# A stack of four graph-attention layers: the minimum over adj moved, a's columns scaled on GpSimd and fetched first, the last batch finished one tile at a time

## The chip, the cores and the metric

The kernel runs on one core of a Trainium2 chip. A core has five engines with instruction queues of their own: TensorE (PE in the profile; its weight loads are PEld), VectorE (DVE), ScalarE (ACT), GpSimd (POOL) and SyncE (SP), which here issues nearly all transfers. Each engine works through its queue in order and waits on semaphores that the others raise. The metric is the time of the whole launch on the device in microseconds, the median of several runs. Less is better.

## The reference

Input x has 32 batches of 512 nodes with 256 features, in float32; adj is a 512 x 512 matrix of int32, zeros and ones in these inputs, with ones on its diagonal. Four layers follow one another, each added to x:

```python
h = relu(layernorm(x)); x = x + L0(h, adj, W, a)   # one head, slope 0.2, elu
h = relu(layernorm(x)); x = x + L1(h, adj, W, a)   # one head, slope 0.01, relu
h = relu(layernorm(x)); x = x + L2(h, adj, W, a)   # four heads of 64, slope 0.2, elu
h = relu(layernorm(x)); x = x + L3(h, adj, ...)    # see below

# what each attention computes
Wh  = h @ W
e   = leaky_relu(Wh @ a[:F] [:, None] + Wh @ a[F:] [None, :], slope)
e   = where(mask, e, -inf)          # L0: adj > 0 or i == j; L1, L2: adj != 0; L3's last: adj > 0
out = softmax(e, -1) @ Wh           # then elu or relu

# L3
o = relu(h @ mlp1_w + mlp1_b)                     # 256 -> 512
o = elu(elu(gat(o, no mask, W_fc, a_fc))) + o     # all 512 nodes with all
r = relu(o @ mlp2_w + mlp2_b)                     # 512 -> 256
L3 = relu(elu(elu(gat(r, adj > 0, W_hand, a_hand))) + r)
```

In every masked layer a node attends to the nodes that adj names; since the inputs have no negative entries in adj and a full diagonal, one mask serves all layers. (In the reference elu is applied inside gat and again after it.)

## The kernel before

**Two programs.** `fast` computes everything under the assumptions that adj has no negative entry, that its diagonal is positive, and that no exponential grows too large. It leaves a flag. Each engine then loads that flag (L1187) and branches at L1188; only when the flag is set does the slower function `general` compute the output anew. In these runs the flag is clear. Three numbers make up the flag: the minimum over adj (L225 and L226, into `differ[:, 0:1]`), the minimum over the diagonal (L228 and L229), and the largest exponential seen in any batch (`seen`, filled by `note` at L305).

**Layout.** The 512 nodes are four tiles of 128 rows (`NT = 4`), features lie in the free dimension. The exponential of a leaky ReLU of a sum is written as a product: three extra columns beside each W (the columns of `a` projected through W, scaled by slope - 1 and by 1 - slope) give per-node factors, so that a weight is max(row factor, column factor) times the mask. `weights` (L342) makes the four 128 x 512 tiles of weights on VectorE at L352; `aggregate` (L380) multiplies them with the values on PE; a column beside the values (each node's own factor) yields the denominator, and `reciprocal` (L384, instruction at L386) inverts it. The products are float32; PE works through one in two records of the profile.

**Loading.** `load_x` (L93) fetches a batch. `fetch_w` (L128) fetches a weight matrix and calls `fetch_a` (L99), which fetches the two halves of the vector `a` as columns of single floats: two transfers for each layer, issued on SP at L103. SP's order at the start is x of batch 0 (L150), W0 and then its `a` (L151), adj (L153), x of batches 1 to 3, and then the other weights. `finish_w` (L137) scales the columns of `a` (`scale_a`, L109: two instructions on VectorE, for W0, W1, WFC and WHA) and then projects them through W (`project`, L113: transposes on PE, a copy `wT` on ScalarE at L120, small products with `a`, and a copy into the spare columns of W on VectorE at L126).

**The mask.** `setup` (L206) is a generator whose pieces are placed among the first pieces of the batches. It compares adj with zero into `own` (L209, VectorE), puts ones on the diagonal (L210, affine_select on GpSimd), turns the 16 blocks on PE (L218) and stores `maskT` (L219, ScalarE). Then come W1's columns, the minimum over adj, the diagonal's minimum, the columns of W2 (`A`, L231 and L232), WFC's columns, two triangles (`before`, `after`) and the band of ties that a sort uses (L239 to L250), and WHA's columns.

**Order.** Four batches run interleaved (`NS = 4`). Each is a generator (`batch`, L729) that yields a due time after each piece, and the loop at L754 always takes the piece that is due first. A scheduler of the framework then places each engine's instructions by its own estimates of time; `keep_in_program_order` ties an instruction to its place. So program order is not the order of the queues: the triangles' memsets, for instance, stand in VectorE's queue ahead of batch 0's statistics.

**The end of a batch.** `layer3` (L689) ends with a loop over pairs of tiles (`t0` = 0 and 2). For both tiles of a pair the attention's average is taken (`averages`, L396), its exponential and its ReLU are written into the two halves of `q` and `y` (L698, L699), then `elu2_plus1` (L407) makes the double elu over the whole pair: a min on VectorE (L409), an exp on ScalarE (L410), a sum on VectorE (L411). The residual `rT` is transposed on PE into a bank and added (L709, VectorE), ReLU follows (L710, ScalarE), then the addition to x (L712, GpSimd) and the transfer of two tiles to the output (L713, SP, 256 KB). In batches 0 to 30 other batches' work surrounds this; in the last batch nothing follows it but the flag (L774 to L783).

Of the kernel before, what the change touches and what calls it, by code (L numbers as in the profile page):

```python
# [24 lines left out]
OP = mybir.AluOpType  # L25
AX = mybir.AxisListType

EPS = 1.0e-5
P = 128
# [6 lines left out]
def fast(ctx, tc, flag, x, adj, w0, a0, w1, a1, w2, a2, mlp1_w, mlp1_b, mlp2_w, mlp2_b,  # L36
         w_fc, a_fc, w_hand, a_hand, out):
    nc = tc.nc
    B, N, F = x.shape
    NT = N // P  # L40
# [27 lines left out]
    def transpose(p, x, i, tied=False):  # L68
        spent[0] += 2 * P
        instruction = nc.tensor.transpose(p, x, i)  # L70
        if tied:
            tc.keep_in_program_order(instruction)
# [4 lines left out]
    def bank():  # L77

        own = [turn[0], *(i for i in range(NS) if i not in active and i != turn[0])]
        banks[0] += 1  # L80
        return psum.tile([P, N], FP, tag=f"b{own[banks[0] % len(own)]}", name="b", bufs=8 // NS)
# [11 lines left out]
    def load_x(b):  # L93
        t = work.tile([P, NT, F], FP, tag="x", name="x", bufs=NS + 1)
        nc.sync.dma_start(t, x[b].rearrange("(t p) f -> p t f", p=P))
        return t


    def fetch_a(a, name):  # L99
        ft = a.shape[0] // (2 * P)  # L100
        t = const.tile([P, ft, 3], FP, name=name)
        for s, c in ((0, 2), (1, 0)):
            nc.sync.dma_start(  # L103
                t[:, :, c:c + 1],
                a[s * ft * P:(s + 1) * ft * P, :].rearrange("(t p) o -> p t o", p=P),
            )
        return t

    def scale_a(t, alpha):  # L109
        nc.vector.tensor_scalar_mul(t[:, :, 1:2], t[:, :, 0:1], alpha - 1.0)  # L110
        nc.vector.tensor_scalar_mul(t[:, :, 2:3], t[:, :, 2:3], 1.0 - alpha)

    def project(dst, block, k, a_cols):  # L113

        ft, n = a_cols.shape[1], a_cols.shape[2]
        p = bank()
        for f in range(ft):
            transpose(p[:, f * P:(f + 1) * P], block(k, f), ident)
        wT = work.tile([P, N], FP, tag="y", name="wT", bufs=3)
        nc.scalar.copy(wT[:, :ft * P], p[:, :ft * P])  # L120
        q = bank()
        for f in range(ft):
            matmul(
                q[:, :n], wT[:, f * P:(f + 1) * P], a_cols[:, f, :], start=(f == 0), stop=(f == ft - 1)
            )
        nc.vector.tensor_copy(dst, q[:, :n] if len(dst.shape) == 2 else q[:, :n].rearrange("p (h c) -> p h c", c=3))  # L126

    def fetch_w(w, a, name):  # L128

        kt, cols = w.shape[0] // P, w.shape[1]  # L130
        t = const.tile([P, kt, cols + 3], FP, name=name)
        wr = w.rearrange("(k p) f -> p k f", p=P)
        for c in range(0, cols, F):
            nc.sync.dma_start(t[:, :, c + (3 if c else 0):c + (3 if c else 0) + F], wr[:, :, c:c + F])
        return t, fetch_a(a, name + "a")

    def finish_w(fetched, alpha):  # L137
        t, a_cols = fetched

        def block(k, f):  # L140
            c = f * P + (3 if f * P >= F else 0)
            return t[:, k, c:c + P]

        scale_a(a_cols, alpha)
        for k in range(t.shape[1]):
            project(t[:, k, F:F + 3], block, k, a_cols)
            yield


    xts = {0: load_x(0)}  # L150
    W0, _ = fetched0 = fetch_w(w0, a0, "W0")  # L151
    adj_sb = work.tile([P, NT, N], I32, tag="w", name="adj", bufs=4)
    nc.sync.dma_start(adj_sb, adj.rearrange("(t p) j -> p t j", p=P))  # L153
    for b in range(1, NS):
# [1 line left out]
    W1, _ = fetched1 = fetch_w(w1, a1, "W1")  # L156
# [6 lines left out]
    for h in range(NH):  # L163
        t, r = divmod(h * D, P)
# [8 lines left out]
    WFC, _ = fetched3 = fetch_w(w_fc, a_fc, "WFC")  # L173
    WM2 = const.tile([P, KH, F], FP, name="WM2")
    nc.sync.dma_start(WM2, mlp2_w.rearrange("(k p) f -> p k f", p=P))
    WHA, _ = fetched4 = fetch_w(w_hand, a_hand, "WHA")
# [23 lines left out]
    differ = const.tile([P, 2], FP, name="differ")  # L200
# [5 lines left out]
    def setup():  # L206

        own = work.tile([P, NT, N], FP, tag="w", name="own", bufs=4)
        nc.vector.tensor_scalar(own, adj_sb, 0.0, None, op0=OP.is_gt)  # L209
        nc.gpsimd.affine_select(  # L210
            out=own, in_=own, pattern=[[P, NT], [-1, N]], base=0, channel_multiplier=1,
            compare_op=OP.not_equal, fill=1.0,
        )
        for j in range(NT):
            turn[0] = NS - 1 - j % (NS - 1)
            p = bank()
            for t in range(NT):
                transpose(p[:, t * P:(t + 1) * P], own[:, t, j * P:(j + 1) * P], ident, j + t == 0)  # L218
            nc.scalar.copy(maskT[:, j, :], p)  # L219
        turn[0] = NS - 1  # L220
        yield
        yield from finish_w(fetched1, 0.01)


        tc.keep_in_program_order(nc.vector.tensor_reduce(differ[:, 0:1], adj_sb, AX.XY, OP.min))  # L225
        nc.vector.tensor_scalar(differ[:, 0:1], differ[:, 0:1], 0.0, None, op0=OP.is_lt)  # L226
        least = small([1], "rden")
        nc.vector.tensor_reduce(least, diag, AX.X, OP.min)  # L228
        nc.vector.tensor_scalar(differ[:, 1:2], least, 0.0, None, op0=OP.is_le)  # L229
        nc.vector.tensor_copy(W2[:, :, :, :D], raw2.rearrange("p k (h d) -> p k h d", d=D))  # L230
        nc.vector.tensor_scalar_mul(A2v[:, :, 1:2], A2v[:, :, 0:1], -0.8)  # L231
        nc.vector.tensor_scalar_mul(A2v[:, :, 2:3], A2v[:, :, 2:3], 0.8)  # L232
        for k in range(KF):
            project(W2[:, k, :, D:], lambda k, f: raw2[:, k, f * P:(f + 1) * P], k, A2)
            yield
        yield from finish_w(fetched3, 0.2)

        for tri, sign in ((before, 1), (after, -1)):
            nc.vector.memset(tri, 1.0)  # L239
            nc.gpsimd.affine_select(  # L240
                out=tri, in_=tri, pattern=[[sign, P]], base=0, channel_multiplier=-sign,
                compare_op=OP.is_gt, fill=0.0,
            )
        ties = work.tile([P, 2 * N - P], FP, tag="w", name="ties", bufs=4)
        nc.vector.memset(ties, TINY)
        nc.gpsimd.affine_select(
            out=ties, in_=ties, pattern=[[-1, 2 * N - P]], base=N - P, channel_multiplier=1,
            compare_op=OP.is_gt, fill=0.0,
        )
        nc.vector.tensor_copy(band, ties)  # L250
        yield
        yield from finish_w(fetched4, 0.2)
# [3 lines left out]
    def small(shape, name):  # L256
        return work.tile([P] + shape, FP, tag=name, name=name, bufs=2 * NS)
# [33 lines left out]
    def turned(xn, when):  # L291

        hT = work.tile([P, KF, N], FP, tag="hT", name="hT", bufs=3)
        turn_pair(xn, hT, 0)
        yield when
        turn_pair(xn, hT, 2)
        yield after_us(0.6)
        return hT
# [78 lines left out]
    def pair(tag="y"):  # L377
        return work.tile([P, 2, F], FP, tag=tag, name=tag, bufs=3)
# [17 lines left out]
    def averages(v, wt, t):  # L396
        p = bank()
        aggregate(p[:, :F + 1], wt, t, lambda j: v[:, j, :F + 1])
        return p[:, :F], reciprocal(p[:, F:F + 1])
# [289 lines left out]
    def layer3(xt, xn, when, b):  # L689
        oT = yield from linear_t((yield from turned(xn, when)), WM1, b1, "oT", 2)  # L690
        yield from (attend if b >= B - 1 else sort_attend)(oT, b)
        rT = yield from linear_t(oT, WM2, b2, "rT", 2)
        v, wt = yield from plain(rT, WHA)
        for t0 in range(0, NT, 2):
            y, q = pair(), pair("q")
            for i in range(2):
                p, rd = averages(v, wt, t0 + i)
                nc.scalar.activation(q[:, i, :], p, AF.Exp, scale=rd)  # L698
                nc.scalar.activation(y[:, i, :], p, AF.Relu, scale=rd)  # L699
                yield after_us(0)  # L700
            elu2_plus1(y, q)
            p = bank()
            for i in range(2):
                for k in range(KF):
                    transpose(
                        p[:, (i * KF + k) * P:(i * KF + k + 1) * P], rT[:, k, (t0 + i) * P:(t0 + i + 1) * P], ident
                    )
            yf = y.rearrange("p a f -> p (a f)")
            nc.vector.scalar_tensor_tensor(yf, p, -1.0, yf, op0=OP.add, op1=OP.add)  # L709
            nc.scalar.activation(y, y, AF.Relu)  # L710
            xr = xt[:, t0:t0 + 2, :]
            nc.gpsimd.tensor_tensor(xr, xr, y, op=OP.add)  # L712
            nc.sync.dma_start(  # L713
                out[b, t0 * P:(t0 + 2) * P, :].rearrange("(t p) f -> p t f", p=P), xr
            )
            yield after_us(0)

# [36 lines left out]
    while ready:  # L754
        i = min(ready, key=ready.get)
# [23 lines left out]
    p = bank()  # L779
# [437 lines left out]
```

## Time and profile before

| | |
|---|---|
| median of 3 runs | 2943.76 us (2943.12 to 2945.2) |
| the profiled run, whole | 2945.59 us |
| span of the profile | 2943.9 us |
| mean granted clock of TensorE | 0.995 |
| adj landed; own (L209) begins | 10.99 us |
| own's affine_select on GpSimd (L210) | 12.29, for 1.91 us |
| first transposes of WFC on PE | 28.77 us |
| last of the output transfers (256 KB each) issued | 2938.5 us |

All times in the trace are microseconds from the start of the span. A line of the timeline gives start, duration, engine, line of the kernel, operation, output and inputs by their names, and in brackets how long the engine had been idle before it and what released it. The page's chain is followed back from the last instruction: at each step to whatever released it, or to the instruction before it in the same queue; its lines give the share of the span that each engine or line holds on this chain. The start and the end of the span differ from its middle in that few batches are under way: from 10 to 20 us PE is busy for 8.6 of 10 us, and after 2932 us for 0.4 us in all.

### The profile page before, as it was taken

How to read it: one execution, taken by the hardware profiler on the slowest of the kernel's cores; microseconds unless marked ns; L12 is line 12 of the kernel's file. 1: busy time of each engine (PE TensorE's matmuls, PEld its weight loads, DVE VectorE, ACT ScalarE, POOL GpSimd, SP SyncE). 2: the span in 40 equal slices, each digit the busy share in tenths (PEclk: the TensorE clock that was granted, in tenths of full speed). 3: DMA queues.
4: the chain of work that ended last, by engine and by line, in shares of the span. 5: the costliest groups of instructions: out<-in, count | busy, mean ns of one | idle time of the engine just before them, and what ended most of it. 6: DMA issues, size and time to landing. Idle time of an engine off the chain costs nothing.

```text
span 2943.9 us, 43065 instructions
## 1 busy us (share of the span) xinstructions
PE 2863.2 (97%) x15177; PEld 2326.1 (79%) x15177; DVE 2224.0 (76%) x5674; ACT 1537.4 (52%) x3918; POOL 501.3 (17%) x509
## 2 busy tenths in 40 slices
PE   7999999999999999999999999999999999999988
PEld 6777888877887877888878888778888788887766
DVE  4677877778877778878777878777777788787764
ACT  4444455554555554555554555545555555555544
POOL 0011112111122111122021121121221111221120
PEclk9999999999999999999999999999999999999999
DMA  3033223233223233233332232332232322332230
GB/s 94 19 101 99 87 83 116 92 96 99 90 87 105 95 98 98 83 102 98 98 101 90 86 107 93 96 99 89 87 116 89 99 95 81 101 112 77 96 106 23
DMA packets 193150, 270.89 MB, mean 92 GB/s; under 512 B 16992, under 2 KB 156062, under 8 KB 192928
## 3 DMA queue, kind: packets, MB, share of 16 engines
q1 hardware_dynamic: 163168, 169.76, 18.5%
q0 software_dynamic: 29760, 98.30, 10.1%
q8 instruction: 123, 2.02, 0.3%
q14 instruction: 99, 0.81, 0.1%
HBM read 152.62 MB, written 115.39 MB: 91 GB/s over the span
## 4 chain that ended last, share of the span: by engine, by line
PE 77%; DVE 13%; ACT 5%; DMA 3%; issue 1%; POOL 0%; SPq 0%; POOLq 0%; ACTq 0%; DVEq 0%
PE b L66 70%; PE b L70 7%; DVE st L268 3%; DVE xn L279 1%; DMA order<-v,at 1%; DVE xn L275 1%; DVE sums L640 1%; DVE w L352 1%; ACT v L324 1%; DMA sums<-order 1%; DVE sums L631 1%; ACT y L504 1%; DVE x L405 1%; ACT q L503 1%; DVE y L404 1%
## 5 line engine op out<-in xcount | busy, mean ns | idle before, releaser
L66 PE MATMUL b<-v,w 128*128 128x65 f32 (+1 forms) x7232 | 1222.4, 321 | 6.8 <-DVE w L352 6.7
L66 PEld LDWEIGHTS b<-v,w 128*128 128x128 f32 x7232 | 1053.6, 192 | 167.8 <-issue 64.2
L66 PE MATMUL b<-WFC,oT 128*128 128x256 f32 (+1 forms) x2048 | 496.3, 380 | 0.0
L66 PEld LDWEIGHTS b<-WFC,oT 128*128 128x128 f32 x2048 | 373.6, 189 | 48.7
L66 PE MATMUL b<-W,hT 128*128 128x259 f32 (+1 forms) x1536 | 382.0, 387 | 9.2 <-ACT hT L289 4.4
L352 DVE SCALAR_TENSOR_TENSOR w<-b,v,maskT 128x512 f32<-128x512 f32 x512 | 369.0, 743 | 4.9 <-PE b L70 3.6
L606 POOL DMA_INDIRECT order<-v,at x248 | 284.2, 1146 | 491.2 <-DVE oT L725 152.0
L66 PEld LDWEIGHTS b<-W,hT 128*128 128x128 f32 x1536 | 283.0, 190 | 58.9 <-ACT v L324 8.9
L352 DVE SCALAR_TENSOR_TENSOR w<-spread,v,maskT 128x512 f32<-128x512 f32 x384 | 269.3, 741 | 0.0
L386 DVE RECIPROCAL rden<-b 128x1 f32<-128x1 f32 (+1 forms) x516 | 78.7, 164 | 246.5 <-PE b L66 243.2
L712 POOL TENSOR_TENSOR x<-x,y 128x512 f32<-128x512 f32 x64 | 81.3, 1270 | 1074.9 <-ACT y L710 963.8
L66 PE MATMUL b<-hT,WM 128*128 128x512 f32 x512 | 248.6, 596 | 0.7 <-ACT hT L289 0.7
L654 POOL DMA_INDIRECT g<-table,at x124 | 120.9, 975 | 724.8 <-ACT y L674 385.3
L66 PE MATMUL b<-oT,WM 128*128 128x512 f32 x512 | 230.3, 592 | 0.0
L528 ACT ACTIVATE v<-b,ends 128x256 f32<-128x256 f32 x256 | 118.6, 466 | 176.7 <-PE b L66 172.4
L268 DVE BATCH_NORM_STATS2 st<-x 128x6 f32<-128x256 f32 x512 | 192.7, 408 | 5.1 <-DMA x<-in_x_dram 2.6
L289 ACT ACTIVATE hT<-b 128x512 f32<-128x512 f32 x256 | 147.0, 590 | 83.8 <-PE b L70 83.8
L338 ACT ACTIVATE oT<-b,bias 128x512 f32<-128x512 f32 x128 | 87.7, 685 | 193.2 <-PE b L66 193.2
L411 DVE TENSOR_TENSOR y<-q,y 128x512 f32<-128x512 f32 x192 | 132.5, 690 | 67.0 <-ACT q L410 66.5
L70 PE MATMUL b<-ident,xn 128*128 128x128 f32 x1024 | 152.7, 279 | 23.5 <-DVE xn L279 20.9
L66 PEld LDWEIGHTS b<-oT,WM 128*128 128x128 f32 x512 | 97.0, 190 | 95.1 <-issue 91.8
L70 PEld LDWEIGHTS b<-ident,xn 128*128 128x128 f32 x1024 | 121.9, 143 | 60.6 <-DVE xn L279 33.8
(142 smaller groups left out, 3738.3 us busy)
## 6 DMA issues: line engine op xcount, KB each, us to landing
table<-sums SPq DMA_DIRECT2D x62, 1032.0 KB
sums<-order SPq DMA_DIRECT2D x62, 516.0 KB
spread<-row SPq DMA_DIRECT2D x96, 256.0 KB
x<-in_x_dram SPq DMA_DIRECT2D x32, 512.0 KB
out_dram<-x SPq DMA_DIRECT2D x64, 256.0 KB
sums<-order SPq DMA_DIRECT2D x62, 129.0 KB
order<-v,at POOLq DMA_INDIRECT x248
g<-table,at POOLq DMA_INDIRECT x124
```

What stands on the lines that cost most here:

```text
L66: nc.tensor.matmul(p, w, x, **flags)
L70: instruction = nc.tensor.transpose(p, x, i)
L268: nc.vector.bn_stats(st[:, i, :], xt[:, t0 + i, :])
L289: nc.scalar.activation(hT[:, :, t0 * P:(t0 + 2) * P], p.rearrange("p (k n) -> p k n", k=KF), AF.Relu)
L338: nc.scalar.activation(o[:, f, :], p, AF.Relu, bias=bias[:, f:f + 1])
L352: w = nc.vector.scalar_tensor_tensor(wt[:, j, :], r, t_col(j), maskT[:, j, :], op0=OP.max, op1=OP.mult)
L386: nc.vector.reciprocal(r, den)
L411: nc.vector.tensor_tensor(r, q, r, op=OP.add)
L528: nc.scalar.activation(halves[c][:, t, :F], ps[:, :F], AF.Copy, scale=ends[:, t, 0:1])
L606: nc.gpsimd.indirect_dma_start(out=orders[c], out_offset=bass.IndirectOffsetOnAxis(ap=at[:, 0, t:t + 1], axis=0), in_=halves[c][:, t, :], ...
L654: nc.gpsimd.indirect_dma_start(out=g, out_offset=None, in_=table, in_offset=bass.IndirectOffsetOnAxis(ap=at[:, 1, t:t + 1], axis=0),)
L712: nc.gpsimd.tensor_tensor(xr, xr, y, op=OP.add)
```

## The change

Four edits. The minimum over adj is taken directly behind the comparison that makes `own`, in program order, and not behind W1's columns. The scaling of the columns of `a` goes from VectorE to GpSimd for W0, W1, WFC and WHA (A's two, for W2, stay). `a0` is fetched before x of batch 0 and before W0, and `fetch_w` takes it ready-made. In the last batch the closing loop takes one tile at a time and adds to x on VectorE; the output leaves in four transfers of 128 KB instead of two of 256 KB. All other batches keep the loop over pairs.

```diff
     def scale_a(t, alpha):
-        nc.vector.tensor_scalar_mul(t[:, :, 1:2], t[:, :, 0:1], alpha - 1.0)
-        nc.vector.tensor_scalar_mul(t[:, :, 2:3], t[:, :, 2:3], 1.0 - alpha)
+        nc.gpsimd.tensor_scalar_mul(t[:, :, 1:2], t[:, :, 0:1], alpha - 1.0)
+        nc.gpsimd.tensor_scalar_mul(t[:, :, 2:3], t[:, :, 2:3], 1.0 - alpha)
...
-        return t, fetch_a(a, name + "a")
+        return t, fetch_a(a, name + "a") if len(a.shape) == 2 else a
...
+    a0_sb = fetch_a(a0, "W0a")
     xts = {0: load_x(0)}
-    W0, _ = fetched0 = fetch_w(w0, a0, "W0")
+    W0, _ = fetched0 = fetch_w(w0, a0_sb, "W0")
     adj_sb = work.tile([P, NT, N], I32, tag="w", name="adj", bufs=4)
     nc.sync.dma_start(adj_sb, adj.rearrange("(t p) j -> p t j", p=P))
...
             compare_op=OP.not_equal, fill=1.0,
         )
+        tc.keep_in_program_order(nc.vector.tensor_reduce(differ[:, 0:1], adj_sb, AX.XY, OP.min))
+        nc.vector.tensor_scalar(differ[:, 0:1], differ[:, 0:1], 0.0, None, op0=OP.is_lt)
         for j in range(NT):
...
         yield from finish_w(fetched1, 0.01)
 
 
-        tc.keep_in_program_order(nc.vector.tensor_reduce(differ[:, 0:1], adj_sb, AX.XY, OP.min))
-        nc.vector.tensor_scalar(differ[:, 0:1], differ[:, 0:1], 0.0, None, op0=OP.is_lt)
         least = small([1], "rden")
...
         v, wt = yield from plain(rT, WHA)
-        for t0 in range(0, NT, 2):
-            y, q = pair(), pair("q")
-            for i in range(2):
+
+        n = 1 if b == B - 1 else 2
+        for t0 in range(0, NT, n):
+            y, q = pair()[:, :n, :], pair("q")[:, :n, :]
+            for i in range(n):
                 p, rd = averages(v, wt, t0 + i)
                 nc.scalar.activation(q[:, i, :], p, AF.Exp, scale=rd)
                 nc.scalar.activation(y[:, i, :], p, AF.Relu, scale=rd)
                 yield after_us(0)
             elu2_plus1(y, q)
             p = bank()
-            for i in range(2):
+            for i in range(n):
                 for k in range(KF):
                     transpose(
                         p[:, (i * KF + k) * P:(i * KF + k + 1) * P], rT[:, k, (t0 + i) * P:(t0 + i + 1) * P], ident
                     )
             yf = y.rearrange("p a f -> p (a f)")
-            nc.vector.scalar_tensor_tensor(yf, p, -1.0, yf, op0=OP.add, op1=OP.add)
+            nc.vector.scalar_tensor_tensor(yf, p[:, :n * F], -1.0, yf, op0=OP.add, op1=OP.add)
             nc.scalar.activation(y, y, AF.Relu)
-            xr = xt[:, t0:t0 + 2, :]
-            nc.gpsimd.tensor_tensor(xr, xr, y, op=OP.add)
+            xr = xt[:, t0:t0 + n, :]
+            (nc.gpsimd if n == 2 else nc.vector).tensor_tensor(xr, xr, y, op=OP.add)
             nc.sync.dma_start(
-                out[b, t0 * P:(t0 + 2) * P, :].rearrange("(t p) f -> p t f", p=P), xr
+                out[b, t0 * P:(t0 + n) * P, :].rearrange("(t p) f -> p t f", p=P), xr
             )
             yield after_us(0)
```

## The prediction

> **What bounds the kernel now.** I read the page first (busy shares, then the chain that ended last), then the timelines of the first 60 and last 45 us, then PE's windows cut at the steps of its clock, because the order of instructions told me where to look. That order, compared on each engine, is unchanged from some 45 us to some 2926 us apart from names. Only the two ends can differ.
>
> ```profile
> span 2943.9 us, 43065 instructions
> PE 2863.2 (97%) x15177; PEld 2326.1 (79%) x15177; DVE 2224.0 (76%) x5674; ACT 1537.4 (52%) x3918; POOL 501.3 (17%) x509
> PE 77%; DVE 13%; ACT 5%; DMA 3%; issue 1%; POOL 0%; SPq 0%; POOLq 0%; ACTq 0%; DVEq 0%
> ```
>
> The middle is PE's stream. Work on VectorE or GpSimd counts only where PE waits for it, and what the start gains is kept if the rest of the chain moves as one. The timeline of the start has such a place:
>
> ```profile
> 23.41 0.32 PE L70 MATMUL b<-ident,v 128*128 128x128 f32 x1
> 23.47 2.28 DVE L225 TENSOR_REDUCE differ<-adj 128x1 f32<-128x2048 int32 x1
> 25.66 2.72 DVE L352 SCALAR_TENSOR_TENSOR w<-b,v,maskT 128x512 f32<-128x512 f32 x4
> 26.46 2.94 PE L66 MATMUL b<-v,w 128*128 128x257 f32 x6 [2.73 <-DVE w L352]
> ```
>
> The last transpose ends at 23.73. The minimum over adj (L225) stands ahead of the weights w (L352), whose first tile PE needs, so PE is idle for 2.73 us. The windows of PE show the second price (busy us, then the granted clock, then DMA):
>
> ```profile
> 18.66:22.08 3.42, 2.92 (x20) 1.00 0.68 166
> 22.08:25.49 3.41, 1.61 (x8) 1.00 1.14 321
> 25.49:28.90 3.41, 2.44 (x6) 0.50 0.99 209
> 28.90:32.32 3.42, 3.42 (x14) 0.50 0.53 156
> 32.32:35.73 3.41, 3.41 (x19) 1.00 0.02 5
> 59.62:63.04 3.42, 2.04 (x12) 1.00 0.02 5
> ```
>
> After the stretch with the gap (1.61 us busy) PE gets half clock for two stretches of 3.41 us; a stretch with 2.04 us busy lost nothing. The end, from the chain in order of time and the timeline:
>
> ```profile
> 2930.17 0.17 DVE rden L386
> 2932.58 1.26 POOL x L712
> 2932.89 1.23 DVE L409 TENSOR_SCALAR q<-q 128x512 f32<-128x512 f32 x1 [0.17 <-ACT q L698]
> 2934.16 0.72 ACT L410 ACTIVATE q<-q,minus 128x512 f32<-128x512 f32 x1 [0.94 <-DVE q L409]
> 2934.98 0.69 DVE L411 TENSOR_TENSOR y<-q,y 128x512 f32<-128x512 f32 x1 [0.80 <-ACT q L410]
> 2935.71 0.69 DVE L709 SCALAR_TENSOR_TENSOR y<-b,y 128x512 f32<-128x512 f32 x1
> 2936.49 0.63 ACT L710 ACTIVATE y<-y 128x512 f32<-128x512 f32 x1 [1.61 <-DVE y L709]
> 2937.20 1.26 POOL L712 TENSOR_TENSOR x<-x,y 128x512 f32<-128x512 f32 x1 [3.36 <-ACT y L710]
> ```
>
> PE's last product ends at about 2931.9. What follows is a serial chain of pair-wide steps (two tiles of rows each); the output DMA is issued at 2938.49. L409 took 1.23 us beside GpSimd's add, against 0.43 in the mean.
>
> **What the Trainium skill says.** "TensorE: Matmul & The Clock Gate", Part 1 (The HAM clock gate): activity is watched in free-running windows of 3413 ns and the clock is halved after an idle one. The trace agrees on half clock and on 3.41 us; it shows in addition that 1.61 us of work in a window is too little. "SBUF — State Buffer", Who interferes with whom: VectorE and GpSimd share a port pair under an exclusive lock; tensor_scalar can enter a mode that needs it, tensor_reduce never does on trn2. The 1.23 us above fit the first; no run here shows a reduce beside GpSimd. "DMA: Bandwidth & Descriptors", Specifications: transfers under 512 B fall below line rate. W0a's two loads are columns of single floats; issued at 1.86 and 2.37, they released L111 and L110 only at 6.96 and 8.32.
>
> **1. The minimum moved (own, L209, now directly precedes it in the program).** On VectorE it now follows the two copies of W's columns, which end at 12.37. VectorE's next instruction there waited until 16.35 for W1a, and with the scaling gone the next is the copy of raw at 16.92. 2.28 + 0.15 us fit into 4.5, so it costs nothing; without that cover it would delay PE by up to 2.3 us. It runs beside GpSimd's affine_select of own (12.29 to 14.2), which PE waits for at 14.26: bound 0 (no lock) to +2.2 (full lock), taken as 0 by the skill's sentence.
> At 23.56 w is then free to start once its bank is complete, about 23.75 instead of 25.66: 1.9 us. PE starts 0.81 us after w does (51.85 to 52.66 elsewhere), at 24.56. PE's gap falls from 2.73 to about 0.8 us, so the stretch has over 2.4 us of work and I expect full clock. Walking forward: w's four tiles come every 0.67 us, each full-clock product takes 0.45 us (two records of 0.226), so the first output tile ends at 27.0. Then follow what before did by 33.3: two more products (0.9), A's four (0.9), four transposes (0.44), ending at 29.2. Gain 4.1 us: 1.9 from the wait and about 2.2 from the clock. Of the half clock's 2.85 us, 0.65 is given back since PE now waits for w's later tiles.
> Late next: the first reciprocal, through the band's copy and the diagonal's minimum. ties' memset ends at 27.5, affine_select (0.93) at 28.5, band at 29.6, reciprocal at 29.75 against 33.77: a shift of 4.0. The diagonal's DMA, issued at 26.64, must have landed by 29.6; the DMA share is down to 0.06 by 29.0. PE moves four WFC transposes behind the products, same count, nothing.
>
> **2. a's scaling on GpSimd.** Eight instructions of 0.16 us leave VectorE, none on the chain except as waits. GpSimd's price for 2 or 4 columns: 0.19 (its copy of ends, 62 times) to 0.75 us (the same copy once); I take 0.3. W1a follows own (14.2) and its DMA (16.3): done by 17 to 17.9, needed at 19.48. WFCa and WHAa stand behind ties; done by 29.1 to 31.5, WFCa needed at 32.2. Hidden. W0a stands ahead of the triangles and own, and lands long before 12.29.
>
> **3. First a fetched first.** Two issues (0.98 us) move ahead of x and W; adj stays fifth at 2.88. x is issued at 1.81 instead of 0.83 and lands about 5.4 instead of 4.41. VectorE's four tiles take 4.2 us there including 1.8 of waits for W0a, which go, so xn ends by about 9 as before (9.45). But own waits for adj (10.99), and the DMA engines, full from 2.4 on, start the large loads 1.0 us later, less the 0.4 us that the small ones cost in the stretch of 4.5 to 5.0 (128 GB/s instead of 350). Bound: 0 to +1.2; taken +0.5, all on the path.
>
> **4. Last batch tile by tile.** PE turns three of the four residual tiles beforehand instead of two: +0.22 us in a gap of 0.45, hidden. VectorE and ScalarE get twice the instructions at half width. Estimated per 128x256, from the rows: VectorE 0.42 (two inputs, L496) or 0.3 (tensor_scalar), ScalarE 0.47 from PSUM (L698), 0.5 for L410, 0.42 for L710 (0.72 and 0.63, less 0.2). The order on VectorE puts tile 1's add and tile 3's reciprocal ahead of tile 2's min. Following both queues: tile 1's add ends 2932.5, reciprocal 2932.7, tile 2's min 2933.0, the flag 2933.35, tile 3's min 2933.6, exp (behind ScalarE's relu) 2934.4, sum 2934.9, residual 2935.35, relu 2935.8, add 2936.27, DMA issue 2936.3. Against 2938.49: 2.2 us. The last DMA is half as large (128 KB, at 330 GB/s 0.4 us less); half of that is taken because the branch after it may end last: 0.2. GpSimd's add of 1.26 becomes one of 0.42, and the lock on L409 goes.
>
> **Sum.** -4.1 + 0.5 - 2.2 - 0.2 = -6.0 us: the profiled span 2943.9 becomes 2937.9, its run 2945.59 becomes 2939.6. Against the median of 2943.76 this is 2937.8. The runs themselves spread over 2.1 us.
>
> **Rivals.**
> A (the forecast, 0.57): 2937.8, its own range 2935.5 to 2940.
> B, the clock is not won (0.24): the gap closes, but a window falls on the remaining idle time and the half clock comes again, or adj's landing takes it back. For it: 2.44 us busy at half clock did not lift it. Against: 2.04 us at full clock did not lower it. Then 1.9 - 0.5 + 2.4 = 3.8: 2940.
> C, more is won (0.13): half clock occurs twice more, at 76.6 (one window) and 2831 (three). The phase of the windows against the work decides; one window is worth up to 1.7 us. 2932.5 to 2936. Against: the shift of 3.6 us is nearly one window, so the pattern should repeat.
> D, slower (0.06): the same mechanism against us. The stream is shifted against the windows, and thin stretches that escaped (2.04 and 2.29 us busy near 60 and 105) fall under. Each costs up to 1.7 us; from four such windows on (6.0 / 1.7) the gain is gone, with five it is 2946.
> That the change doesn't do what it says is excluded for the order; the order shows the reduce, scaling and adds where they are meant to be.
>
> **How the numbers follow.** About 0.2% (5.9 us, below 2937.9) is what a measurement can tell from no change. A lies on that line: half of it (0.28) and C give faster 0.41; I put 0.45, for the tail may profit from less crowding on GpSimd. Same is the rest of A and B, less what went to faster: 0.49; slower D, 0.06. The range 2933.5 to 2942 leaves out D and the outer part of B and C.
>
> **What would show it.** In the start: w at about 24.2, PE's gap under 1 us, no 0.50 in the clock before 70 us, the chain at 45 us some 3.6 earlier. If own starts later than 12.2 the loads are to blame; if affine_select takes over 3 us, the reduce locks it. At the end: 4.4 us from PE's last product to the output's issue. Wrong if the clock halves again after 25 us, or if the last products themselves come at another distance from the start than before.

## The result, and the profile after

The changed kernel took 2939.43 us (median of 11 runs, 2930.69 to 2942.47), the kernel before 2944.21 us (11 runs, 2941.33 to 2946.87) beside it. The ratio is 0.9979, with a 95% interval of 0.9971 to 0.9987: 6.2 us faster, between 3.8 and 8.5. The profiled run is the slowest of the 11 (2942.47 us, span 2940.8), so its span shows less of the gain than the median. The page of after begins:

```profile
span 2940.8 us, 43083 instructions
PE 2866.2 (97%) x15177; PEld 2328.4 (79%) x15177; DVE 2224.9 (76%) x5676; ACT 1539.6 (52%) x3922; POOL 498.6 (17%) x515
PE 79%; DVE 12%; ACT 5%; DMA 2%; issue 1%; SPq 0%; POOL 0%; POOLq 0%; ACTq 0%; DVEq 0%
```

PE was busy 3 us longer for the same 15177 records: some of them ran at half clock that had not before. VectorE lost a point of the chain and PE gained two. The timeline of after's start (line numbers are one to four higher than before's):

```profile
11.07 1.23 DVE L210 TENSOR_SCALAR own<-adj 128x2048 f32<-128x2048 int32 x1 [2.14 <-DMA adj<-in_adj_dram]
12.35 2.28 DVE L215 TENSOR_REDUCE differ<-adj 128x1 f32<-128x2048 int32 x1
12.37 1.92 POOL L211 TENSOR_SCALAR_AFFINE_SELECT own<-own 128x2048 f32<-128x2048 f32 x1 [7.92 <-DVE W L126]
...
23.86 2.73 DVE L353 SCALAR_TENSOR_TENSOR w<-b,v,maskT 128x512 f32<-128x512 f32 x4 [0.21 <-PE b L70]
24.66 2.87 PE L66 MATMUL b<-v,w 128*128 128x257 f32 x12 [0.84 <-DVE w L353]
...
31.26 0.16 DVE L229 TENSOR_REDUCE rden<-diag 128x1 f32<-128x4 int32 x1 [1.92 <-DMA diag<-in_adj_dram]
33.01 1.02 PE L66 MATMUL b<-WFCa,wT 128*128 128x3 f32 x8 [1.10 <-issue]
```

The reduce runs beside affine_select and neither slows the other: 2.28 and 1.92 us, against 2.28 and 1.91 apart. w starts 1.8 us earlier, PE waits 0.84 us for it instead of 2.73, and the products of v and w run at full clock. Then VectorE waits 1.92 us for the diagonal's load, with the first reciprocal queued behind it, and PE pauses for 1.10 us.

The windows of after, cut where its clock changes (busy us and count of PE, PEld, DVE, ACT, POOL; granted clock; DMA share; GB/s):

```profile
22.21:25.63 3.42, 2.53 (x12) 1.84 (x12) 2.10 (x5) 1.19 (x4) 0.00 (x0) 1.00 1.08 303
...
32.46:35.87 3.41, 2.57 (x22) 2.36 (x22) 1.45 (x3) 2.51 (x6) 0.00 (x0) 1.00 0.01 3
35.87:39.28 3.41, 3.41 (x11) 2.85 (x12) 1.55 (x7) 1.52 (x4) 0.00 (x0) 0.50 0.00 0
39.28:42.70 3.42, 2.95 (x26) 2.66 (x24) 1.45 (x5) 1.50 (x4) 0.00 (x0) 1.00 0.00 0
42.70:46.11 3.41, 3.41 (x11) 2.53 (x11) 1.31 (x6) 0.47 (x3) 0.00 (x0) 0.50 0.00 0
46.11:49.52 3.41, 3.36 (x11) 2.22 (x11) 0.68 (x4) 1.78 (x6) 0.00 (x0) 0.50 0.00 0
```

The half clock that before had from 25.5 to 32.3 is gone, but three new stretches of it follow, after windows in which PE was busy for 2.57 and 2.95 of 3.41 us. PE's 100th record starts 4.4 us earlier than in before's profile, its 200th 0.7 us later.

The end, in after's timeline:

```profile
2931.49 5.29 SPq L716 DMA_DIRECT2D out_dram<-x  x4
2932.18 0.27 PE L70 MATMUL b<-ident,bad 128*1 128x128 f32 x1
...
2933.37 0.29 DVE L410 TENSOR_SCALAR q<-q 128x256 f32<-128x256 f32 x1
2934.64 0.42 DVE L412 TENSOR_TENSOR y<-q,y 128x256 f32<-128x256 f32 x1
2935.09 0.42 DVE L712 SCALAR_TENSOR_TENSOR y<-b,y 128x256 f32<-128x256 f32 x1
2935.43 0.99 DVE L715 TENSOR_TENSOR x<-x,y 128x256 f32<-128x256 f32 x2
2935.54 0.42 ACT L713 ACTIVATE y<-y 128x256 f32<-128x256 f32 x1 [0.38 <-DVE y L712]
```

The half-width steps take what the prediction gave them (0.29, 0.42, 0.42). From PE's last record (which ends at 2932.45) to the end of the span it is 8.3 us; in before it was 11.5 (2932.41 to 2943.9). So in this pair of profiles PE ends at the same time, and the 3.1 us between the two spans are all the tail's. The distance hardly varies: 8.3 to 8.4 us in the eight profiles with the new tail, 11.5 to 11.9 in the six with the old. The tail is worth 3.1 to 3.6 us.

About one microsecond of this lies behind the issue of the last output transfer: from there to the end of the span it is 4.3 us in after and 5.4 in before. GpSimd's last instructions, before's first and then after's, show one reason (count, then shortest, median and longest in ns, then the start of the first and of the last):

```profile
L1213 POOLq DRAIN  x3: 40/107/4485, 2938.6 to 2943.6; - x3
```

```profile
L1216 POOLq DRAIN  x3: 40/107/4489, 2934.3 to 2940.5; - x3
```

The first of these DRAINs takes 4.49 us. In before it begins 0.1 us behind GpSimd's last addition to x and ends at 2943.06, 0.8 us before the end of the span; SP, which waits for the output to land, is through at 2942.8, almost together with it. In after the additions of the last batch are VectorE's, GpSimd's DRAIN is over at 2938.84, and SP is the last, at 2939.9. So two things had to end earlier, the transfer and GpSimd's work; no run separates them.

### The profile page after: what moved, and what is told of

The parts are those of the page before. It is cut to its first block, busy times and chain, and to the rows that moved or that the text cites. A ratio compares the mean times of both kernels' runs of the same rounds, so it can differ in the third digit from the quotient of the medians.

```text
span 2940.8 us, 43083 instructions
## 1 busy us (share of the span) xinstructions
PE 2866.2 (97%) x15177; PEld 2328.4 (79%) x15177; DVE 2224.9 (76%) x5676; ACT 1539.6 (52%) x3922; POOL 498.6 (17%) x515
## 3 DMA queue, kind: packets, MB, share of 16 engines
q1 hardware_dynamic: 163200, 169.76, 18.5%
## 4 chain that ended last, share of the span: by engine, by line
PE 79%; DVE 12%; ACT 5%; DMA 2%; issue 1%; SPq 0%; POOL 0%; POOLq 0%; ACTq 0%; DVEq 0%
PE b L66 72%; PE b L70 7%; DVE st L269 3%; DVE xn L280 1%; DVE xn L276 1%; DVE sums L641 1%; ACT v L325 1%; DVE sums L632 1%; DVE x L406 1%; DVE mv L270 1%; DVE y L405 1%; ACT rs L272 1%; DVE y L712 1%; ACT y L505 1%; ACT q L504 1%
## 5 line engine op out<-in xcount | busy, mean ns | idle before, releaser
L412 DVE TENSOR_TENSOR y<-q,y 128x512 f32<-128x512 f32 (+1 forms) x194 | 132.9, 685 | 67.0 <-ACT q L411 66.5
```

Of the source, the lines that this page charges most:

```text
L412: nc.vector.tensor_tensor(r, q, r, op=OP.add)
```

## The experiments

Twelve runs in three groups: nine new kernels, and before, the changed kernel and `no_first` once more. Each group was measured on a chip of its own and shares its runs of the kernel before (medians 2941.52, 2941.12 and 2940.87 us). Ratios are to these, and only ratios are compared between groups.

**Group 1: the halves of the change, and two waits.** `tail_only` is before with the closing loop of the change and nothing else. `start_only` is before with the other three edits.

> Only the last edit (last batch by tiles, VectorE's add). Theory (the profile of after: from PE's last product to the end of the span 8.7 us instead of 12.0): 3.3 us less than before, about 2940.9, with the spread of before, since the start is untouched. Rival (the tail's steps were hidden behind the flag and the branch, and the whole change acts through the start): under 1 us less.

> The first three edits without the last. Theory (4.4 us are won by PE's 100th product, then given back to the wait for the diagonal's load and to windows of half clock that follow it): the median 1 to 2 us less than before, runs spread over some 10 us as after's do, the best near 2934. Rival (the start's gain is absorbed by loads that do not move, whatever the clock does): the median within 0.5 us of before and no wider spread than before.

Measured: tail_only 0.9990 [0.9981, 0.9998], 2.9 us faster; start_only 0.9990 [0.9982, 0.9998], also 2.9 us. Each half is a gain, though both intervals end just short of 1.

`diag_early` is the changed kernel with the diagonal's load issued before the large weights of the MLP:

```diff
+    diag = const.tile([P, NT], I32, name="diag")
+    with nc.allow_non_contiguous_dma(reason="vectors onto partitions"):
+        nc.sync.dma_start(diag, adj.rearrange("i j -> (i j)")[::N + 1].rearrange("(t p) -> p t", p=P))
     WM1 = const.tile([P, KF, H], FP, name="WM1")
...
-    diag = const.tile([P, NT], I32, name="diag")
...
-        nc.sync.dma_start(diag, adj.rearrange("i j -> (i j)")[::N + 1].rearrange("(t p) -> p t", p=P))
```

> After, with the diagonal's load issued behind A's columns instead of near the end of the weights' loads. Theory: the first reciprocal comes 1.5 to 2 us earlier than 31.34, PE's pause of 1.1 us before WFCa goes, its stretch is no longer thin, the half clock at 35 us is rarer: 2 to 3 us less than after, about 2937, fewer runs above 2940. Rival (some other load or queue is late anyway): within 1 us of after.

Measured: 0.9982 [0.9975, 0.9989]. The diagonal's minimum ran at 27.33 without waiting, and PE's pause fell from 1.10 to 0.64 us. But half clock came all the same, from 41.4 us on, and the ratio is that of the changed kernel (0.9979): no gain from this wait can be seen.

`before_warm` is before with 20 transposes of no use on PE in the gap of 2.73 us:

```diff
+    warm = [1]
...
+            if warm:
+                warm.clear()
+                d = psum.tile([P, N], FP, tag="b3", name="warm", bufs=8 // NS)
+                for i in range(20):
+                    tc.keep_in_program_order(nc.tensor.transpose(d[:, :P], ident, ident))
```

> Before, with 20 transposes more on PE in its gap of 2.73 us; their result is read by nobody. Theory (half of the 4.1 us was the clock): the gap stays, no half clock from 25 to 32 us, about 2.2 us less than before: 2942. Rival (the half clock comes from something other than PE's idle time, or costs nothing): 2944, or up to 0.5 more.

Measured: 0.9993 [0.9984, 1.0001]. Its profile has no half clock before 71.5 us, while all four profiles with the gap left empty have it between 22 and 32 us: what PE did in the gap was the cause of the half clock there. Against a profile of before from group 2 (`before_again`), PE's 60th record, ahead of the gap, starts 0.56 us later and its 120th 2.16 us earlier: filling the gap won 2.2 to 2.7 us, where the prediction had put the clock's part at 2.2. In the time, the gain of 2.1 us can't be told from none.

**Group 2: the order of the loads.** The four profiles of group 1 split by one thing: own starts at 8.80 and 9.05 us where a0 is fetched behind W0, at 11.06 and 11.17 where it is fetched first. `no_first` is the changed kernel with a0 fetched as before; `first_only` is before with a0 fetched first; `best` is no_first with the diagonal's minimum taken behind WFC's columns; `before_again` is the kernel before.

```diff
-    a0_sb = fetch_a(a0, "W0a")
     xts = {0: load_x(0)}
-    W0, _ = fetched0 = fetch_w(w0, a0_sb, "W0")
+    W0, _ = fetched0 = fetch_w(w0, a0, "W0")
```

> The changed kernel with a0 fetched behind x and W0 again, as before; only the order of the first five transfers on SP differs from the changed kernel. Theory 'a first delays adj': own (the comparison of adj) starts about 2 us earlier than in the changed kernel (about 9.0 instead of 11.1 us), the stream of PE follows it by as much, and the time is about 2 us below the changed kernel's, ratio to before 0.9972. Rival 'adj's landing differs from launch to launch whatever the order': own between 9 and 11 us, time that of the changed kernel, ratio 0.9979, within 1 us.

> The kernel before with only a0 fetched ahead of x and W0. Theory 'a first delays adj': own at about 11 us, some 2 us later than the kernel before on the same chip, and the time 1 to 2 us above it, ratio 1.0005. What the prediction took for this edit: +0.5 us, ratio 1.0002. Rival 'landing differs whatever the order': ratio 1.0000, own where before has it.

> The changed kernel with a0 fetched as before and the minimum over the diagonal taken behind WFC's columns, so that the first reciprocal no longer stands behind a load of 2 KB in single words. If both hold (a first costs 2 us, the wait for the diagonal 1 to 2 us): some 3 to 4 us below the changed kernel, ratio to before 0.9968, and PE's pause ahead of WFC's first transposes under 0.5 us. Rival: what is won by 30 us is given back by half clock and later waits anyway, so that the ratio is that of the changed kernel, 0.9979.

> The kernel before once more, for its profile beside the others of this chip. Theory 'a first delays adj': own starts at 8.8 to 9.1 us here, as in the two kernels of this chip that fetch a0 behind W0. Rival 'landing differs from launch to launch': anywhere from 8.8 to 11.1 us.

Measured: first_only 1.0011 [1.0003, 1.0019], 3.2 us slower; no_first 0.9975 [0.9969, 0.9982], 7.3 us faster; best 0.9973 [0.9962, 0.9984]. The timeline of before_again, then that of first_only:

```profile
5.78 0.17 DVE L111 TENSOR_SCALAR W0a<-W0a 128x2 f32<-128x2 f32 x1
...
8.80 1.23 DVE L209 TENSOR_SCALAR own<-adj 128x2048 f32<-128x2048 int32 x1 [1.32 <-DMA adj<-in_adj_dram]
```

```profile
3.47 0.17 DVE L110 TENSOR_SCALAR W0a<-W0a 128x2 f32<-128x2 f32 x1 [0.33 <-DMA W0a<-in_L_gnn_a_dram]
5.71 0.75 DVE L269 BATCH_NORM_STATS2 st<-x 128x6 f32<-128x256 f32 x2 [2.06 <-DMA x<-in_x_dram]
...
11.13 1.23 DVE L210 TENSOR_SCALAR own<-adj 128x2048 f32<-128x2048 int32 x1 [2.21 <-DMA adj<-in_adj_dram]
```

And the traffic of the first 12 us in 40 slices, before_again first, then first_only:

```profile
GB/s 0 0 0 0 0 0 68 160 341 372 379 365 219 348 302 106 220 315 396 341 273 375 416 410 372 304 263 318 375 375 379 365 365 375 372 348 348 348 355 341
```

```profile
GB/s 0 0 0 0 0 0 1 2 2 22 55 177 328 386 375 324 324 376 283 178 171 157 218 259 259 348 212 358 362 372 399 396 389 386 376 386 372 355 348 341
```

With a0 first the large loads reach 300 GB/s about 1.2 us later (slice 12 instead of 8, counted from 0), and a second dip (171, 157, 218) comes at 6 to 7 us. By 12 us, 2.79 MB have moved instead of 3.30; at 350 GB/s that is 1.5 us. The adj load lands 2.3 us later. Why the dip is longer isn't shown.

best, whose first reciprocal stands behind no load, isn't measurably faster than no_first; but no_first's own wait for the diagonal was only 0.33 us, so little was left to take away.

**Group 3: the minimum alone, the changed kernel beside no_first, and the clock.** `after_again` and `no_first_again` are what they say. `min_only` is before with the two lines of the minimum moved:

```diff
+        tc.keep_in_program_order(nc.vector.tensor_reduce(differ[:, 0:1], adj_sb, AX.XY, OP.min))
+        nc.vector.tensor_scalar(differ[:, 0:1], differ[:, 0:1], 0.0, None, op0=OP.is_lt)
         for j in range(NT):
...
-        tc.keep_in_program_order(nc.vector.tensor_reduce(differ[:, 0:1], adj_sb, AX.XY, OP.min))
-        nc.vector.tensor_scalar(differ[:, 0:1], differ[:, 0:1], 0.0, None, op0=OP.is_lt)
```

`warm_wfc` is no_first with useless transposes ahead of WFC's small products (in `project`):

```diff
         q = bank()
+        for f in range(3 if ft == NT else 0):
+            nc.tensor.transpose(q[:, P:2 * P], ident, ident)
         for f in range(ft):
             matmul(
```

> The changed kernel, for its time beside the other kernels of this chip. If fetching a first costs what the kernel before with this edit alone lost (3.2 us): 2 to 4 us above the changed kernel without it (no_first_again), ratio to before 0.9983, own at 11.1 us. If the edit is worth nothing: ratio 0.9975, as the one without it had.

> The changed kernel with a0 fetched as before, beside the changed kernel itself. Theory 'a first delays adj': own at 8.9 us and 2 to 4 us below the changed kernel, ratio 0.9973. Rival: the same time as the changed kernel within 1 us.

> The kernel before with the minimum over adj moved and nothing else (scaling on VectorE, a behind W0, the last batch in pairs). The prediction's first step: 4.1 us won by some 29 us, w's wait of 2.73 us down to 0.85, own's affine_select 1.9 us as before, no half clock from 22 to 30 us, ratio 0.9986 if it is kept. Rival 'the next thin stretch takes half of it back': the half clock comes at 35 to 45 us instead, some 1.5 to 2.5 us are kept, ratio 0.9993.

> no_first with 12 transposes of no use on PE (three ahead of each group of products of WFC with its a, 128 columns each). They change nothing of the result. Theory 'the clock follows the columns that stream through PE in 3.41 us, and halves below about 1540': the stretch of 31 to 38 us then carries about 1650 columns instead of 1160 per 3.41 us, no half clock before 68 us, PE's 200th product 1 us or more earlier than in no_first although 1.3 us of work were added; time 1 to 2 us below no_first's at most. Rival 'the half clock there has another cause': half clock at 35 to 46 us again, PE 1 us later, time 1 us above no_first's.

Measured: after_again 0.9977 [0.9968, 0.9987], no_first_again 0.9972 [0.9960, 0.9983], with medians of 2933.86 and 2934.20 us: beside the rest of the change, the cost of a first can't be told from nothing in the times, though own starts at 11.23 against 8.91. min_only 0.9993 [0.9983, 1.0004]: the gain of 2.1 us can't be told from none. warm_wfc 0.9966 [0.9955, 0.9978], 10 us faster than before: the best of all kernels run, though its interval still overlaps those of after_again and no_first_again.

The times of the single edits don't add up to the whole: min_only (-2.1), first_only (+3.2) and tail_only (-2.9) make -1.8 us, against the -6.2 and -6.8 measured for the changed kernel. Each has an interval of 2.4 to 3.1 us to either side, so the gap may be spread alone; but the scaling on GpSimd was in no run alone.

Where a launch gains and loses is seen when the start of PE's n-th record is set against that of before_again (worked out from the traces, us; the added transposes not counted):

```
record           120th    160th    200th    280th    400th
min_only         -4.14    -4.14    -1.85    -1.86    -0.19
first_only       +2.53    +2.53    +2.53    +2.53    +2.53
start_only       -1.94    -1.94    -1.93    -1.93    -3.59
after_again      -1.48    -1.48    -1.49    -1.49    -3.14
no_first_again   -3.37    -3.37    +0.44    +0.43    -1.23
warm_wfc         -2.88    -1.85    -3.44    -3.45    -5.10
```

Up to the 160th record (40 us) the parts add up: -4.14 and +2.53 make -1.61, between start_only's -1.94 and after_again's -1.48. In the changed kernel, a first costs 1.9 us there (-1.48 against -3.37). Behind the 160th record each launch goes its own way, in steps of half-clock windows, and one profile of each can't tell these launches from their kernels: at the 14000th record tail_only is 2.6 us ahead of before_again, with the same program up to there. The windows of min_only:

```profile
23.80:27.23 3.43, 3.43 (x23) 3.08 (x22) 2.61 (x10) 0.00 (x0) 0.93 (x1) 1.00 0.86 186
...
34.05:37.46 3.41, 3.08 (x26) 2.77 (x24) 1.74 (x7) 1.81 (x7) 0.00 (x0) 1.00 0.00 0
37.46:40.88 3.42, 3.28 (x10) 2.49 (x10) 1.39 (x5) 0.58 (x3) 0.00 (x0) 0.50 0.00 0
40.88:44.29 3.41, 3.36 (x11) 2.13 (x10) 0.75 (x4) 1.77 (x6) 0.00 (x0) 0.50 0.00 0
```

A window with 3.08 us of work is followed by half clock, while before's window at 59.62 with 2.04 us was not. What the busy time consists of explains it. PE's groups in after from 32.46 to 35.87 us, then in before from 59.62 to 63.04:

```profile
L66 PE MATMUL b<-WFCa,wT 128*128 128x3 f32 x14 | 1.9, 259 | 1.4 <-issue 1.1 <-ACT wT L120 0.3
L70 PE MATMUL b<-ident,WFC 128*128 128x128 f32 x8 | 1.1, 277 | 0.0
```

```profile
L66 PE MATMUL b<-W,hT 128*128 128x268 f32 x4 | 1.2, 415 | 0.8 <-ACT hT L289 0.8
L70 PE MATMUL b<-ident,xn 128*128 128x128 f32 x6 | 1.0, 282 | 0.6 <-DVE xn L275 0.6
L66 PE MATMUL b<-v,w 128*128 128x257 f32 x2 | 0.6, 380 | 0.0
```

The first streams 14 x 3 + 8 x 128 = 1066 columns, the second 4 x 268 + 6 x 128 + 2 x 257 = 2354, or some 1830 if the records on its edges count by their share. A product of 3 columns keeps PE busy for about 0.12 us and streams next to nothing. warm_wfc was the test: with 128 more columns from each of its 12 transposes, its windows over the same work are

```profile
28.58:31.99 3.41, 3.41 (x28) 3.12 (x26) 0.45 (x4) 2.90 (x7) 0.02 (x1) 1.00 0.39 133
31.99:35.41 3.42, 3.17 (x22) 2.89 (x22) 2.97 (x10) 0.96 (x3) 0.00 (x0) 1.00 0.00 0
35.41:38.82 3.41, 3.11 (x29) 2.80 (x27) 1.39 (x5) 2.56 (x7) 0.00 (x0) 1.00 0.00 0
38.82:42.23 3.41, 3.27 (x24) 2.82 (x24) 2.09 (x10) 1.62 (x7) 0.00 (x0) 1.00 0.00 0
```

The clock stays full with 3.11 to 3.17 us of work, hardly more than min_only's 3.08; its whole profile has one half-clock window (at 2803.6 us) before the idle end. The useless work costs it 1.5 us by the 160th record, and by the 200th it is 3.9 us ahead of no_first_again. By their share, the windows at 31.99 and 35.41 carry over 1900 columns each; 768 of those in the second are six useless transposes. One profile wouldn't be enough: two of the eight others with the minimum moved have no half clock between 35 and 50 us either. The mean granted clock over all runs points the same way: 0.998 in warm_wfc's 7 against 0.996 in no_first_again's 7 and 0.997 in after_again's 10.

## Why the prediction was right, and where its steps were not

The forecast sum of -6.0 us lies beside the measured -6.2, within rival A's range. That it lies so close is in part luck. The steps beneath the sum are right in part, errors of both signs stand against each other, and what the prediction had named as a sign of being wrong came true in the profiled run: the clock halves again after 25 us.

- **The minimum (step 1): right in size.** Forecast -4.1 us by 29 us; min_only shows -4.14 on PE's 120th record, 2.2 to 2.7 of which are the clock's part by before_warm. In min_only's time it isn't shown (-2.1 us [-5.0, +1.2]). No lock with affine_select, PE's gap 0.84, no half clock between 22 and 32 us in any of the nine profiles with the minimum moved, while all four of before, before_again, tail_only and first_only have it there.
- **"No 0.50 clock before 70 us": wrong.** In six of those nine profiles half clock comes between 35 and 50 us and takes 2.3 to 4.0 us back, from the 120th to the 200th record. In the profiled run the stream, forecast 3.6 us earlier at 45 us, is 0.7 us later than before's at the 200th record. The step that failed is the measure of a thin window. The prediction judged windows by busy time and called 2.4 us enough; the windows that fell there had up to 3.08 us of it, much of it in products of 3 columns. Rival B's mechanism thus acts in most launches, beside A's.
- **The windows' phase: wrong.** Against C it was argued that a shift of nearly one window would repeat before's pattern. The pattern isn't a property of the program: before_again has half clock at 176 and at 2811 us, where before's first profile has none.
- **First reciprocal at 29.75: wrong in the profiled run (31.34), about right elsewhere (30.14 in after_again).** The condition on the diagonal's load was named; the load landed at 31.2 in one launch and near 30.0 in the other. Taking the wait away brought nothing measurable (diag_early, best).
- **Scaling on GpSimd (step 2): right as far as the profile goes.** 0.21 to 0.23 us each, once 0.67; done by 30 us. What it is worth wasn't measured alone.
- **a first (step 3): mis-sized.** Taken +0.5, at most +1.2. Own starts 11.06 to 11.23 us in the five profiles with a0 first, 8.52 to 9.05 in the eight profiles of the experiments with it behind W0: 2.3 us on average, +2.5 on PE's stream alone and +1.9 beside the other edits, +3.2 [0.9, 5.6] in first_only's time. The one profile of before at hand had own at 10.99 and waited for W0a until 6.96 and 8.32 us, where in those eight profiles both halves had landed by 6.7: it was unlike them, and against it the change showed no delay. Whether the launch or the chip was the reason isn't shown; before's median was 2944.2 us in that measurement, and 2940.9 to 2941.5 in the three groups.
- **The tail (step 4): right in the steps, too small behind them.** Forecast 4.4 us from PE's last product to the output's issue, measured 4.3. The 0.2 for the smaller last transfer was about 1.0: from issue to the end of the span 4.3 us instead of 5.4. The prediction priced GpSimd's shorter addition but put the DRAIN of 4.49 us behind it at nothing. In all 3.2 us instead of 2.4; tail_only's 2.9 [0.6, 5.6] agrees.

By the profiles, then: -4.1 + 2.5 - 3.2 = -4.8 us, without the half clock that follows after 35 us. This lies in the interval of both measurements of the changed kernel (-6.2 [-8.5, -3.8] and -6.8 [-9.4, -3.8]); no_first's sum without the 2.5 is -7.3 as measured, though its own profile gives 2.4 us back to the clock by the 200th record. What the clock adds differs by launch: among the 11 runs of the changed kernel the two with a mean clock of 0.994 took 2941.4 us on average, the one with 0.998 took 2930.7. The mean over runs is 0.9947 in before (112 runs in the three groups), 0.9955 in the first measurement of the changed kernel and 0.9968 in after_again. But tail_only, whose start is before's, has 0.9954: the idle end runs at half clock (from 2937.1 us in before), so that a shorter end raises the mean by itself. The first measurement thus shows no more clock than the tail explains. How much of the gain is clock can't be settled with these intervals.

## What to carry to other kernels

A stall removed from PE's start is worth its length only until the next thin stretch, so look at how many columns stream through PE per 3.41 us, not at how busy it is; a few useless transposes among tiny products put PE 3.9 us ahead by its 200th record in the one pair of profiles compared, though the gain in the whole time isn't clear of the spread. An edit to the order of loads has to be judged by when the last of the early large loads lands: putting two loads of 1 KB first delayed one of 1 MB by 2.3 us. And take two profiles of the kernel before: the start in the one at hand was 2 us later than in all eight taken afterwards with the same order of loads.

## What was not expected of the hardware

- **The clock follows columns, not busy time.** I added up, for each window of the 14 profiles, the columns of PE's records between 9 and 2915 us. A record on an edge counts by its share; how its end is taken moves a sum by up to some 100. All 42 full-clock windows that were followed by half clock carried 512 to 1537 columns; of some 11800 followed by full clock, only one or two carried fewer than 1550 (the lowest near 1500). Half clock ended after windows with 1522 columns and more, and went on after windows with up to 1569. A record of 257 columns takes 0.226 us, so 3.41 us hold about 3880: for the float32 records of this kernel, the limit lies near 40% of what full clock can stream. This explains the half clock near 70 to 83 us, which comes and goes. A window filled with the heads' products of 65 columns holds 24 records, 24 x 65 = 1560, right at the limit. In ten profiles the window that also holds the wait of about 0.4 us ahead of these products carried 1430 to 1530 columns, and half clock followed. In the other four its edges fell so that it carried over 1650, and the clock stayed full.
- **The start runs at half clock too, and the profile's clock doesn't say so.** The first record of the clock stands at 12.5 to 18.5 us, and before it the views give 1.00. But up to there PE's transposes of 128 columns start 213 ns apart, and 109 ns behind it, in all 14 profiles. The rise follows the first window with more than 1550 columns in each. With a0 first it came at 15.4 to 18.5 us, with a0 behind W0 at 12.5 to 15.3, so that a part of what a launch has lost or won by its 120th record is this clock; the mean clocks given above leave it out.
- "TensorE: Matmul & The Clock Gate", Part 1, says in the Trainium skill that the monitor watches a free-running window and drops the clock after an idle one. The traces agree on free-running and on the length: in each profile the clock's steps lie on a grid of 3.413 us, and the grid's phase differs from launch to launch. But the 42 fallen windows weren't idle: PE was busy for 0.76 to 3.08 us of 3.41.
- **The same program spreads by 5 to 17 us** (5.3 us over after_again's 10 runs, 11.8 over the changed kernel's first 11, 16.5 over min_only's 13), with the granted clock as the visible difference. With intervals of 0.001 to 0.002, differences of 2 us between two kernels can be seen in the first 40 us of their profiles but not in their times.
